# Four edits at handovers of a four-layer macaron kernel: folded matrices, the second pair's answers, choices one turn further apart, rows merged by tile

## The chip, the cores and the metric

The program runs on one core of one Trainium2 chip. The metric is the device time of that core in microseconds (us), lower is better. A core has five engines that each work through a queue of their own in order: PE (matrix products and transposes), DVE (vector work), ACT (activations and copies), POOL (here mostly small element-wise work and the indirect scatters) and SP (which issues most transfers). They meet through semaphores.

## What is computed

x has 4 batches of 512 rows of 128 numbers (2048 rows in all). It goes through four layers, each of the same shape; the two feed-forward halves of a layer share their weights:

```python
for layer in (0, 1, 2, 3):
    x = x + 0.5 * ffn[layer](layernorm(x))
    x = x + attn[layer](layernorm(x))
    x = x + 0.5 * ffn[layer](layernorm(x))
```

The feed-forward parts differ by layer:

- layer 0: a mixture of 8 experts, each row goes to one expert (relu, 512 hidden units); an expert takes the first 320 rows that chose it, later ones get nothing;
- layer 1: sigmoid gates, each row goes to its two best of 8 small experts (64 hidden units each), and to one shared expert;
- layer 2: each row goes to its two best of 8 *linear* experts, `y += gate_e * ((x @ w_in[e].T) @ w_out[e].T)`;
- layer 3: a mixture of 8 experts, each row goes to its two best (relu, 512 hidden units). An expert holds 512 rows; all first choices are ranked ahead of all second choices, so the second choices fill up what the first ones left.

Attention is causal softmax with 16 heads in layers 0 and 1, softmax without a mask in layer 3, and a gated decay over the sequence in layer 2.

## The kernel before

x stays on the chip in four tiles `xs[b]`, one per batch b, each 128 partitions by 4 tiles of 128. Batches are worked on singly or in two **pairs**, [0, 1] and [2, 3]. Many steps are written as generators that `yield` between turns; `skewed(gens, lag)` (L1519) runs several of them in rounds, where generator i joins after i x lag rounds, and so sets the order in which their instructions are written. Outside of a `manual_schedule` block a scheduler in the framework may still move instructions; inside of the one at L1639, POOL keeps the written order. On the chip each engine then takes its instructions strictly in the order of its queue.

**A mixture** (class `Mixture`; f00 and f01 are the two of layer 0, f30 and f31 the two of layer 3) has three steps.

- `tokens(bs, ...)` (L296) normalizes rows (n_f), transposes them (T_f, L195), scores them (lg_f, L330), picks the experts on DVE (from mx_f, L344, on), ranks every row within its expert by matrix products (rank_f, L373), works out addresses (kept, at, slot, to_f, L400 to L409) and has POOL copy the gates beside the rows and scatter them with indirect DMAs, 128 rows each, into one buffer per choice (`disp`, L416).
- `experts(w)` (L426) fetches, for each expert e, its rows d (first choices) and, in layer 3, d2 (second choices). `prepare(e)` (L452) clears in d2 what lies where first choices already fill the slots (a factor `behind` of 0 or 1 per slot), adds d2 to d, transposes d (dT_f, L463) and copies the transposes by ACT. Then come the two products h_f (L487) and o_f (L523), and POOL scatters the answers (L509) into `res`. A row of d or d2 has 128 numbers and 2 more, its row number and its gate.
- `combine(b)` (L533) reads the answers of batch b back (r_f, a DMA on SP's queue) and adds them to `xs[b]` on DVE. The tile r_f comes from a ring of three, tag "n", which the normalized rows of the following stage share.

**Layer 2's matrices.** As the experts of layer 2 are linear, `prep_l2` (L1296) folds w_in[e] and w_out[e] into one 128 x 128 matrix m per expert. The raw weights are fetched while f01's experts run. Then, per expert: four transposes of w_out (wo2T, L1326), a copy to SBUF, four accumulating products with w_in (L1331), a copy into m. Both copies go through the helper `copy` (L131), which alternates between DVE and ACT; in this place all wo2T copies fall to DVE and all copies into m to ACT.

**The first half of layer 1** follows. `combine` of f01 is run for all four batches (L1586), then `followed(pool, bs)` (L1592) for the two pairs, the second 12 rounds behind the first. It calls `l1_ffn(pool, 0, bs)` (L1134): statistics on DVE, rs_f, rstd_f and off_f on POOL, normalized rows n_f on DVE and ACT by turns (`norms`, L160), T_f on PE, its copy nT on ACT, scores lg on PE, two products gu of the shared expert and of one other, the choice of two experts on DVE (`chosen`, L1075, from mx_f to comb), transposes gT of comb, their copy, a DMA of the gate rows to DRAM (rows_f) and one back that spreads them (cb_f), and then per expert h on ACT and DVE, a product with the gates on POOL (L1198) and the product down on PE. For pair 0, `followed` goes on with the start of layer 1's attention.

**Layer 2 and the choices of layer 3.** `behind(pool, bs)` (L1612) runs for each pair the second half of layer 1's feed-forward, all of layer 2, and the choices of f30; the second pair joins 4 rounds later. For pair 1 the two batches' choices are themselves staggered: `skewed([f30.tokens([b], ...) for b in bs], 3)` (L1623), so batch 3 is three turns behind batch 2.

Of the kernel before, what the change touches and what calls it, by code (L numbers as in the profile page):

```python
# [9 lines left out]
FP = mybir.dt.float32  # L10
I32 = mybir.dt.int32
AF = mybir.ActivationFunctionType
ALU = mybir.AluOpType
# [4 lines left out]
P = 128  # L18
D = 128
NB, S = 4, 512  # L20
# [3 lines left out]
E = 8  # L24
# [4 lines left out]
FF = 512  # L29
NC = FF // P  # L30
W = D + 2
# [10 lines left out]
def kernel(ctx: ExitStack, tc: tile.TileContext, a: dict, out: bass.AP):  # L42
    nc = tc.nc
# [12 lines left out]
    def bank(name):  # L56
        return psum.tile([P, 512], FP, name=name, tag="bank", bufs=8)
# [14 lines left out]
    ident = const([P, P], "ident")  # L72
# [58 lines left out]
    def copy(dst, src):  # L131
        n_copies[0] += 1
        if n_copies[0] % 2:
            nc.vector.tensor_copy(dst, src)
        else:
            nc.scalar.copy(dst, src)
# [76 lines left out]
    def bc(ap, shape):  # L213
        while len(ap.shape) < len(shape):
            ap = ap.unsqueeze(len(ap.shape))
        return ap.to_broadcast(shape)
# [28 lines left out]
    class Mixture:  # L245
# [180 lines left out]
        def experts(self, w, beside=None):  # L426

            w1, b1T, w2, b2 = w
            cap, per, whole, left = self.cap, self.per, self.cap // P, self.cap % P
            with tc.tile_pool(name=f"moe_{self.tag}", bufs=2) as pool:  # L430
                if self.k == 2:

                    ps = bank(f"n1_{self.tag}")
# [7 lines left out]
                got, made = {}, {}  # L441
# [10 lines left out]
                def prepare(e):  # L452
                    tag = f"{e}_{self.tag}"
                    d = got[e, 0]
                    if self.k == 2:
                        d2 = got[e, 1]
                        nc.vector.tensor_tensor(d2, d2, bc(behind[:, e, :], [P, per, W]), ALU.mult)
                        nc.vector.tensor_tensor(d[:, :, :D], d[:, :, :D], d2[:, :, 2:], ALU.add)
                        nc.vector.tensor_tensor(d[:, :, D:], d[:, :, D:], d2[:, :, :2], ALU.add)
                    ps = bank(f"dT{tag}")  # L460
                    for s in range(per):
                        m = min(P, cap - s * P)
                        nc.tensor.transpose(ps[:, s * P : s * P + m], d[:m, s, :D], ident[:m, :m])  # L463
                    dT = pool.tile([P, cap], FP, name=f"dT{tag}", tag="dT")
                    nc.scalar.copy(dT, ps[:, :cap])  # L465

                    back = pool.tile([P, per], I32, name=f"back{tag}", tag="back", bufs=8)
                    lost = pool.tile([P, per], FP, name=f"lost{tag}", tag="lost", bufs=4)
                    nc.vector.scalar_tensor_tensor(
                        lost, d[:, :, D], 0.0, astray[:, e * per : (e + 1) * per], ALU.is_equal, ALU.mult  # L470
                    )
                    nc.vector.tensor_tensor(back, d[:, :, D], lost, ALU.add)  # L472
                    made[e] = d, dT, back
# [822 lines left out]
    def prep_l2(pool):  # L1296

        l2["gate"] = load_T(a["L2_ffn_w_gate"], E, D, "gate2T")
        l2["w_in"] = load(a["L2_attn_W_in"], [P, 2 * D], "win2")
        l2["w_out"] = load(a["L2_attn_W_out"], [P, D], "wout2")  # L1300
        l2["b_out"] = load_row(a["L2_attn_b_out"], "bout2")
        l2["b_in"] = load_T(a["L2_attn_b_in"].rearrange("(k d) -> k d", k=2), 2, D, "bin2T")
        yield

        m = pools["w"].tile([P, E, D], FP, name="m2", tag="m2")
        l2["m"] = m
        got = {}

        def fetch(e):
            wi, wo = raw[:, 0, e].rearrange("p (c d) -> p c d", d=D), raw[:, 1, e]  # L1310
            nc.sync.dma_start(wi, a["L2_ffn_w_in"][e].rearrange("(c f) d -> f c d", f=P))
            nc.sync.dma_start(wo, a["L2_ffn_w_out"][e])
            got[e] = wi, wo

        raw = pool.tile([P, 2, E, FF], FP, name="raw2", tag="raw2")
        for e in range(E):

            behind = yield
            nc.gpsimd.tensor_copy(raw[0:1, :, e, 0], behind[0:1, 0:1].to_broadcast([1, 2]))
            fetch(e)  # L1320
        yield
        for e in range(E):
            wi, wo = got[e]
            ps = bank(f"wo2T_{e}")
            for c in range(NC):
                nc.tensor.transpose(ps[:, c * P : (c + 1) * P], wo[:, c * P : (c + 1) * P], ident)  # L1326
            woT = pool.tile([P, FF], FP, name=f"wo2T_{e}", tag="woT", bufs=3)
            copy(woT, ps)
            pm = bank(f"m2_{e}")
            for c in range(NC):  # L1330
                nc.tensor.matmul(  # L1331
                    pm[:, :D], wi[:, c, :], woT[:, c * P : (c + 1) * P], start=(c == 0), stop=(c == NC - 1)
                )
            copy(m[:, e, :], pm[:, :D])

    def l2_ffn(pool, i, bs):
        tag = f"f2{i}_{bs[0]}"
# [93 lines left out]
    l3 = {}  # L1431
# [83 lines left out]
    def whole(parts):  # L1515
        for _ in parts:
            pass

    def skewed(gens, lag):  # L1519

        live = {i: g for i, g in enumerate(gens)}
        r = 0
        while live:
            for i in list(live):
                if r >= i * lag and next(live[i], "end") == "end":
                    del live[i]
            r += 1
            yield
# [46 lines left out]
    with tc.tile_pool(name="weights12", bufs=1) as mid:  # L1575
        pools["w"] = mid
        prep_l1()
        with tc.tile_pool(name="raw2", bufs=1) as pool:
            made = prep_l2(pool)
            next(made)  # L1580
            next(made)
            f01.experts(l0["w"], made.send)
            whole(made)
        first = small.tile([P, 1], FP, name="first_sigmoid", tag="first_sigmoid", bufs=1)
        nc.scalar.activation(first, l2["m"][:, 0, 0:1], AF.Sigmoid)
        for b in range(NB):  # L1586
            whole(f01.combine(b))
        with tc.tile_pool(name="ahead1", bufs=2) as ahead:
            vpads[:] = [padded(ahead, 0), None]
            begun = l1_begin(ahead)  # L1590

            def followed(pool, bs):  # L1592
                yield from l1_ffn(pool, 0, bs)
                if bs[0] == 0:

                    yield from begun[0](0)
                    for g in range(2):
                        begun[1](0, g)
                        yield
                        begun[4][0, g] = begun[2](0, g)  # L1600

            with tc.tile_pool(name="ffn10", bufs=2) as pool:
                whole(skewed([followed(pool, bs) for bs in pairs], 12))

            early = []
            with tc.tile_pool(name="gates10", bufs=1) as pool:
                l1_attn(
                    lambda _: prep_l3_ffn(xs[0]), begun,
                    lambda b: l1_early(pool, pairs[0], early) if b == 1 else iter(()),
                )  # L1610

        def behind(pool, bs):  # L1612
            yield from l1_ffn(pool, 1, bs, early if bs[0] == 0 else None)
            yield from l2_ffn(pool, 0, bs)
            yield from l2_attn(pool, bs)
            yield from l2_ffn(pool, 1, bs)
            if bs[0] == 0:

                parts = f30.tokens(bs, l3["gate"], "scalar", pool, apart=True)
                while next(parts, "end") != "end" and next(parts, "end") != "end":  # L1620
                    yield
            else:
                yield from skewed([f30.tokens([b], l3["gate"], "scalar", pool) for b in bs], 3)  # L1623

        with tc.tile_pool(name="chain", bufs=2) as pool:
            decay = pool.tile([P, S], FP, name="decay", tag="decay", bufs=1)
            nc.gpsimd.memset(decay, 0.9)
            for bs in pairs:
                l2["gates", bs[0]] = pool.tile([P, 2 * NT, P], FP, name=f"gates{bs[0]}", tag=f"gates{bs[0]}", bufs=1)
                nc.gpsimd.memset(l2["gates", bs[0]], 0.0)  # L1630

            l2["row"] = []
            for u in range(E // 4):
                flag = pool.tile([P, 1], FP, name=f"flag{u}", tag=f"flag{u}", bufs=1)
                nc.vector.tensor_reduce(flag, ident.rearrange("p (r c) -> p r c", c=SLOT)[:, :, u], AX.X, ALU.add)
                row = pool.tile([P, P], FP, name=f"row{u}", tag=f"row{u}", bufs=1)
                nc.vector.tensor_copy(row, flag.to_broadcast([P, P]))
                l2["row"].append(row)
            with tc.manual_schedule(engines={mybir.EngineType.Pool}):  # L1639
                whole(skewed([behind(pool, bs) for bs in pairs], 4))  # L1640
        pools["w"] = wpool
# [54 lines left out]
```

## Time and profile before

The time is the median of three runs. One execution was profiled; everything with a time inside the program below is from that one.

| what | value |
|---|---|
| median of 3 runs | 1515.85 us (1512.09, 1516.94, 1515.85) |
| the profiled execution: its own time, its span | 1516.03 us, 1514.3 us |
| mean granted clock of PE in it (1 is full) | 0.914 |
| busy: PE, PE weight loads | 1278.2 us (84%), 817.5 us (54%) |
| busy: DVE, ACT, POOL | 881.6 us (58%), 682.6 us (45%), 696.5 us (46%) |
| moved by DMA | 106.21 MB, 70 GB/s in the mean |

The span is the time between the first and the last instruction in the trace, in which the times of the rows below are counted; the rest of the execution's time lies around it. The rows have two forms. A row of the **chain of waits** is one link of the chain that ended last, in order of time: start in us, length in us, the engine, the operation with its line, and a count; "issue" is time in which an engine stood with nothing that the profile shows to wait for. A row of the **timeline** is one group of like instructions on one engine: start, busy time in us, engine, line, operation, result<-operands, shapes, a count, and in brackets the idle time ahead of it and what ended it. Names without their numbers: n_f can be a row of any mixture or feed-forward part, so the time tells which one it is. The table of **PE in windows of 2 us** has the window and its length, PE's busy time in it with a count of instructions, the clock that PE was granted (1.00 is full speed), the busy share of the DMA engines, and GB/s moved.

### The profile page before, as it was taken

The numbers are of one execution on the slowest core, as the hardware profiler recorded it, in microseconds if no ns is written. First come the engines' busy times: TensorE is split into PE (matmuls) and PEld (weight loads), VectorE is DVE, ScalarE is ACT, GpSimd is POOL, SyncE is SP. The second block draws the span as 40 slices with busy tenths as digits, with TensorE's granted clock in tenths as the row PEclk, the third lists the DMA queues.
The fourth block names the chain that finished last, engine by engine and source line by source line (L and its number), as shares of the span: only waits on it lengthen the run. The fifth ranks groups of instructions, "written<-read, shape, count | busy, mean of one in ns | idle before, by whom it ended". The sixth has DMA issues, their size and how long they took to land.

```text
span 1514.3 us, 28772 instructions
## 1 busy us (share of the span) xinstructions
PE 1278.2 (84%) x10645; PEld 817.5 (54%) x10645; DVE 881.6 (58%) x2893; ACT 682.6 (45%) x1431; POOL 696.5 (46%) x808
## 2 busy tenths in 40 slices
PE   4687999995968989998999878739589999998394
PEld 3464666774755656676656656627333434343273
DVE  5336777663356657777566755434287787772343
ACT  1235877871422367776621222104336555563041
POOL 5346767871533578876443112555520323202253
PEclk9898999996989999999999887759799999998597
DMA  8410240002412874241130000032114000000223
GB/s 259 104 53 22 79 171 11 9 7 78 147 36 57 230 241 151 85 142 36 38 76 1 1 0 3 29 90 85 49 42 149 9 12 5 15 1 15 78 82 108
DMA packets 100660, 106.21 MB, mean 70 GB/s; under 512 B 9084, under 2 KB 73832, under 8 KB 100520
## 3 DMA queue, kind: packets, MB, share of 16 engines
q1 hardware_dynamic: 91752, 90.11, 20.7%
q0 software_dynamic: 6656, 13.22, 2.5%
q8 instruction: 84, 1.38, 0.4%
q10 hardware_dynamic: 2112, 1.05, 0.3%
q14 instruction: 56, 0.46, 0.1%
HBM read 62.49 MB, written 41.85 MB: 69 GB/s over the span
## 4 chain that ended last, share of the span: by engine, by line
PE 66%; DVE 9%; POOL 8%; issue 7%; DMA 6%; ACT 2%; SPq 1%; POOLq 0%; ACTq 0%; DVEq 0%
PE s_a L618 13%; PE t_a L663 8%; PE h_f L487 5%; PE acc_a L757 5%; PE o_f L523 5%; PE acc_a L685 5%; PE y_f L1380 4%; PE t_a L618 3%; PE ot_a L776 2%; POOL disp_f L416 2%; POOL res_f L509 2%; PE gate_f L1397 2%; PE lg_f L330 1%; PE T_f L195 1%; DVE low L707 1%
## 5 line engine op out<-in xcount | busy, mean ns | idle before, releaser
L650 POOL TENSOR_SCALAR sc_a<-sc_a,top_a 128x128 f32<-128x128 f32 (+3 forms) x256 | 276.5, 1096 | 84.4 <-DVE top_a L635 58.5
L618 PE MATMUL s_a<-k_a,q_a 32*128 32x512 f32 (+3 forms) x1536 | 262.7, 540 | 5.4 <-DVE top_a L639 3.5
L727 ACT ACTIVATE w_a<-t_a 128x512 f32<-128x512 f32 x256 | 140.2, 595 | 124.2 <-PE t_a L618 92.1
L707 DVE TENSOR_REDUCE low<-s_a 128x1 f32<-128x512 f32 x256 | 163.4, 684 | 47.8 <-PE t_a L618 34.8
L663 PE MATMUL t_a<-ident,sc_a 128*128 128x128 f32 x1280 | 170.9, 279 | 6.1 <-DVE top_a L639 5.3
L618 PE MATMUL t_a<-ql_a,k_a 32*128 32x512 f32 x512 | 169.7, 648 | 0.5 <-DVE low L707 0.2
L509 POOL DMA_INDIRECT res_f<-y_f,back_f x112 | 109.7, 980 | 127.6 <-ACT y_f L508 91.3
L663 PEld LDWEIGHTS t_a<-ident,sc_a 128*128 128x128 f32 x1280 | 142.1, 142 | 41.2 <-issue 15.6
L652 ACT ACTIVATE sc_a<-sc_a,top_a 128x128 f32<-128x128 f32 (+3 forms) x256 | 134.8, 575 | 13.9 <-DVE top_a L639 13.4
L618 PEld LDWEIGHTS s_a<-k_a,q_a 32*128 32x128 f32 x1536 | 92.0, 185 | 77.7 <-issue 42.5
L672 ACT ACTIVATE w_a<-t_a 128x256 f32<-128x256 f32 (+2 forms) x192 | 94.3, 526 | 68.7 <-PE t_a L663 68.2
L416 POOL DMA_INDIRECT disp_f<-n_f,to_f x96 | 95.1, 991 | 55.8 <-issue 37.1
L523 PE MATMUL o_f<-w_l,h_f 128*128 128x128 f32 (+1 forms) x896 | 110.5, 278 | 1.4 <-ACT h_f L491 1.0
L523 PEld LDWEIGHTS o_f<-w_l,h_f 128*128 128x128 f32 (+1 forms) x896 | 102.3, 184 | 10.3 <-DVE back_f L472 4.4
L487 PE MATMUL h_f<-dT_f,w_l 128*128 128x320 f32 (+1 forms) x256 | 104.0, 544 | 2.8 <-ACT dT_f L465 2.8
L685 PE MATMUL acc_a<-w_a,vpad 128*32 128x128 f32 x2560 | 97.6, 278 | 0.6 <-ACT w_a L672 0.6
L674 ACT COPY w_a<-t_a 128x256 f32<-128x256 f32 (+2 forms) x192 | 93.3, 526 | 5.7 <-PE t_a L663 5.3
L172 POOL TENSOR_SCALAR rs_f<-mv_f 128x4 f32<-128x4 f32 (+1 forms) x23 | 5.3, 232 | 194.8 <-DVE mv_f L169 194.3
L639 DVE CUSTOM_DVE_ANT_0 sc_a<-s_a,future 128x128 f32<-128x128 f32 (+3 forms) x128 | 62.3, 487 | 45.0 <-PE s_a L618 41.4
L639 DVE CUSTOM_DVE_ANT_0 sc_a<-s_a,table 128x128 f32<-128x128 f32 (+3 forms) x128 | 62.5, 488 | 44.0 <-PE s_a L618 33.6
L757 PE MATMUL acc_a<-w_a,vpad 128*32 128x256 f32 x1024 | 84.8, 400 | 2.8 <-ACT w_a L727 1.9
L508 ACT ACTIVATE y_f<-o_f,d_f 128x128 f32<-128x128 f32 (+1 forms) x112 | 39.0, 394 | 103.5 <-DVE o_f L503 92.4
(344 smaller groups left out, 2227.3 us busy)
## 6 DMA issues: line engine op xcount, KB each, us to landing
fac_a<-fac_a_sb SPq DMA_DIRECT2D x36, 256.0 KB
disp_f<-zeros_f SPq DMA_DIRECT2D x4, 2080.0 KB
d_f<-disp_f SPq DMA_DIRECT2D x32, 260.0 KB
w_l<-in_L_ffn_w_dram SPq DMA_DIRECT2D x16, 512.0 KB
cb_f<-rows_f SPq DMA_DIRECT2D x16, 512.0 KB
q_a<-fac_a SPq DMA_DIRECT2D x32, 256.0 KB
k_a<-fac_a SPq DMA_DIRECT2D x32, 256.0 KB
r_f<-res_f SPq DMA_DIRECT2D x16, 256.0 KB
```

The lines of the kernel that those rows point to most:

```text
L416: nc.gpsimd.indirect_dma_start(out=self.to[c][i0 + t][:, :], out_offset=bass.IndirectOffsetOnAxis(ap=to[:, c, t : t + 1], axis=0), in_=ns[ ...
L487: nc.tensor.matmul(ps[u][:, :cap], w1[:, e, (c + u) * P : (c + u + 1) * P], dT, start=True, stop=True)
L509: nc.gpsimd.indirect_dma_start(out=self.back[e * per + s][:, :], out_offset=bass.IndirectOffsetOnAxis(ap=back[:m, s : s + 1], axis=0), in_ ...
L523: nc.tensor.matmul(po[:m, s, :], h[:, c, s * P : s * P + m], w2[:, e, c, :], start=(c == 0), stop=(c == NC - 1),)
L618: nc.tensor.matmul(ps[:, n0:n1], q[r : r + SLOT, i * P : (i + 1) * P], k[r : r + SLOT, n0:n1], start=True, stop=True)
L650: nc.gpsimd.tensor_scalar(sc, sc, top, None, ALU.subtract)
L652: nc.scalar.activation(sc, sc, AF.Exp, bias=top, scale=-1.0)
L663: nc.tensor.transpose(ps[:, x * n + j * P : x * n + (j + 1) * P], st["sc", u, i, r0 + x][:, j * P : (j + 1) * P], ident,)
L685: nc.tensor.matmul(st["acc", u][r * SLOT : (r + 1) * SLOT, i * P : (i + 1) * P], vpads[b % 2][:, j, g * 4 + r, :], st["w", u, i, r][:, j * ...
L707: nc.vector.tensor_reduce(st["low", u][:, i, c : c + 1], ps, AX.X, ALU.max, negate=True)
L727: nc.scalar.activation(w, ps, AF.Exp)
L757: nc.tensor.matmul(acc[r * SLOT : (r + 1) * SLOT, n0:n1], vpads[b % 2][:, j, g * 4 + r, :], st["w", u, j, r][:, n0:n1], start=(j == 0 and ...
```

## The change

There are four edits.

1. In `prepare`, the pass over all of d2 and the add of all of d are replaced by one fused instruction per tile of 128 rows (second row x `behind` + first row), four per expert. The two numbers beside each row are then multiplied and added for themselves.
2. In `prep_l2`, the transposes of expert e are written ahead of the products of expert e - 1, and both copies go to ACT always.
3. `combine` of f01 runs ahead of layer 1 for batches 0 and 1 only; the one for batches 2 and 3 becomes the first two turns of their own `followed`, whose lag is 10 instead of 12.
4. The two staggered choices of f30 in pair 1 are four turns apart instead of three.

```diff
--- before.py
+++ after.py
@@ -454,8 +454,11 @@
                     d = got[e, 0]
                     if self.k == 2:
                         d2 = got[e, 1]
-                        nc.vector.tensor_tensor(d2, d2, bc(behind[:, e, :], [P, per, W]), ALU.mult)
-                        nc.vector.tensor_tensor(d[:, :, :D], d[:, :, :D], d2[:, :, 2:], ALU.add)
+                        for s in range(per):
+                            nc.vector.scalar_tensor_tensor(
+                                d[:, s, :D], d2[:, s, 2:], behind[:, e, s : s + 1], d[:, s, :D], ALU.mult, ALU.add
+                            )
+                        nc.vector.tensor_tensor(d2[:, :, :2], d2[:, :, :2], bc(behind[:, e, :], [P, per, 2]), ALU.mult)
                         nc.vector.tensor_tensor(d[:, :, D:], d[:, :, D:], d2[:, :, :2], ALU.add)
                     ps = bank(f"dT{tag}")
                     for s in range(per):
@@ -1319,19 +1322,23 @@
             nc.gpsimd.tensor_copy(raw[0:1, :, e, 0], behind[0:1, 0:1].to_broadcast([1, 2]))
             fetch(e)
         yield
-        for e in range(E):
-            wi, wo = got[e]
-            ps = bank(f"wo2T_{e}")
-            for c in range(NC):
-                nc.tensor.transpose(ps[:, c * P : (c + 1) * P], wo[:, c * P : (c + 1) * P], ident)
-            woT = pool.tile([P, FF], FP, name=f"wo2T_{e}", tag="woT", bufs=3)
-            copy(woT, ps)
-            pm = bank(f"m2_{e}")
-            for c in range(NC):
-                nc.tensor.matmul(
-                    pm[:, :D], wi[:, c, :], woT[:, c * P : (c + 1) * P], start=(c == 0), stop=(c == NC - 1)
-                )
-            copy(m[:, e, :], pm[:, :D])
+
+        wT = {}
+        for e in range(E + 1):
+            if e < E:
+                ps = bank(f"wo2T_{e}")
+                for c in range(NC):
+                    nc.tensor.transpose(ps[:, c * P : (c + 1) * P], got[e][1][:, c * P : (c + 1) * P], ident)
+                wT[e] = pool.tile([P, FF], FP, name=f"wo2T_{e}", tag="woT", bufs=3)
+                nc.scalar.copy(wT[e], ps)
+            if e > 0:
+                pm = bank(f"m2_{e - 1}")
+                for c in range(NC):
+                    nc.tensor.matmul(
+                        pm[:, :D], got[e - 1][0][:, c, :], wT[e - 1][:, c * P : (c + 1) * P],
+                        start=(c == 0), stop=(c == NC - 1),
+                    )
+                nc.scalar.copy(m[:, e - 1, :], pm[:, :D])
 
     def l2_ffn(pool, i, bs):
         tag = f"f2{i}_{bs[0]}"
@@ -1583,13 +1590,16 @@
             whole(made)
         first = small.tile([P, 1], FP, name="first_sigmoid", tag="first_sigmoid", bufs=1)
         nc.scalar.activation(first, l2["m"][:, 0, 0:1], AF.Sigmoid)
-        for b in range(NB):
+        for b in pairs[0]:
             whole(f01.combine(b))
         with tc.tile_pool(name="ahead1", bufs=2) as ahead:
             vpads[:] = [padded(ahead, 0), None]
             begun = l1_begin(ahead)
 
             def followed(pool, bs):
+                if bs[0] > 0:
+                    for b in bs:
+                        yield from f01.combine(b)
                 yield from l1_ffn(pool, 0, bs)
                 if bs[0] == 0:
 
@@ -1600,7 +1610,7 @@
                         begun[4][0, g] = begun[2](0, g)
 
             with tc.tile_pool(name="ffn10", bufs=2) as pool:
-                whole(skewed([followed(pool, bs) for bs in pairs], 12))
+                whole(skewed([followed(pool, bs) for bs in pairs], 10))
 
             early = []
             with tc.tile_pool(name="gates10", bufs=1) as pool:
@@ -1620,7 +1630,7 @@
                 while next(parts, "end") != "end" and next(parts, "end") != "end":
                     yield
             else:
-                yield from skewed([f30.tokens([b], l3["gate"], "scalar", pool) for b in bs], 3)
+                yield from skewed([f30.tokens([b], l3["gate"], "scalar", pool) for b in bs], 4)
 
         with tc.tile_pool(name="chain", bufs=2) as pool:
             decay = pool.tile([P, S], FP, name="decay", tag="decay", bufs=1)
```

## The prediction

> **What bounds the kernel now.** I read the share line of the chain of waits first, then the chain in order of time at the three places that the change touches, then the timeline there, last PE's granted clock in 2 us windows.
>
> ```profile
> PE 66%; DVE 9%; POOL 8%; issue 7%; DMA 6%; ACT 2%; SPq 1%; POOLq 0%; ACTq 0%; DVEq 0%
> ...
> 438.17 0.44 PE wo2T L1326 x4
> 438.61 2.90 issue
> 441.51 1.13 PE m L1331 x8
> 442.64 1.27 PE T_f L195 x8
> ```
>
> Two thirds of the span are matrix work, which the change leaves alone (no matmul goes or comes). What it can win lies in the handovers. Here, behind the first mixture of layer 0's second half, pair 0's normalized rows end at 436.58 (last of ACT's n_f), but their transposes T_f start at 442.64, behind the last matrix product of layer 2: PE stood 2.90 us for its operand. The timeline says why:
>
> ```profile
> 432.94 1.68 POOL L173 TENSOR_TENSOR rstd_f<-rs_f,mhalf 128x8 f32<-128x8 f32 x1
> ...
> 440.47 0.34 DVE L186 TENSOR_SCALAR n_f<-x,mv_f,rstd_f 128x128 f32<-128x128 f32 x1 [2.33 <-POOL rstd_f L173]
> 440.73 0.68 DVE L134 COPY wo2T<-wo2T 128x512 f32<-128x512 f32 x1
> ```
>
> The copy of the last wo2T stands on DVE behind pair 1's n_f, which waited 2.33 us for POOL. Second place, the last two batches' choices:
>
> ```profile
> 975.89 1.63 PE L195 MATMUL T_f<-ident,n_f 128*128 128x128 f32 x4 [3.04 <-ACT n_f L182]
> 977.31 0.53 PE L373 MATMUL rank_f<-masks_f,not_before 128*128 128x64 f32 x2
> 980.35 0.19 DVE L344 TENSOR_REDUCE mx_f<-lg_f 128x4 f32<-128x32 f32 x1 [1.20 <-PE lg_f L330]
> 981.00 0.17 DVE L409 TENSOR_TENSOR to_f<-slot_f,spare_f 128x8 int32<-128x8 f32 x1
> 982.03 1.12 POOL L416 DMA_INDIRECT disp_f<-n_f,to_f  x1 [6.12 <-DVE masks_f L234]
> ```
>
> Batch 2's rank waits on PE behind batch 3's transposes, its addresses to_f on DVE behind batch 3's mx_f, and POOL, which then issues 16 scatters one after another to 1002.65, starts 6.12 us late. Third, the first expert of layer 3:
>
> ```profile
> 1008.29 0.70 DVE L457 TENSOR_TENSOR d_f<-d_f,behind_f 128x520 f32<-128x520 f32 x1 [3.07 <-DMA d_f<-disp_f]
> 1009.03 0.69 DVE L458 TENSOR_TENSOR d_f<-d_f,d_f 128x512 f32<-128x512 f32 x1
> ...
> 1010.03 1.09 PE L463 MATMUL dT_f<-ident,d_f 128*128 128x128 f32 x4 [23.26 <-DMA d_f<-disp_f]
> ```
>
> Two full passes of DVE run before PE may begin. The second mixture repeats it (1429.07, transposes at 1430.60).
>
> **Part 1: layer 2's matrices and the second pair's answers.** In the new order of instructions, DVE loses eight wo2T copies, and the adds of batches 2 and 3 move behind pair 0's n_f. Between its first add at 425.84 and its last statistic at 432.30, DVE did two of those adds and two of those copies (starts about 0.65 apart, 2.6 us) and waited 0.24 for the fourth answer: the statistics now end near 429.4. POOL needs the same 2.6 us as before (432.30 to off_f at 434.90): n_f from 432.0.
>
> ACT takes the copies: 8 at 0.59 (its nT copy has that size), beside 0.27 for each m, plus the table load of 1.28 after m 0. PE per matrix at full clock: transposes 0.44, products 0.89, so 1.4 us against 2.4 now (418.75, 421.08, 423.46), as the transposes run ahead of the copy. With the table load in front of the third copy (423.2), products 2 to 6 end near 430.7. The last copy stands on ACT behind two n_f and one m: 432.0 + 0.44 + 0.27 + 0.44 = 433.1, copy to 433.7, product 1.1, T_f at 434.85: **7.8 us earlier**.
>
> Given back: the order puts into pair 0's choices (mx at 449.34 to comb at 457.25, 7.9 us) batch 3's add (0.69), four statistics and a new wait. Counted through in that order: mx 0.22, four h products 0.69, the add, eleven steps of about 0.22 and four statistics of 0.26 reach the last mv_f at 7.0; POOL's rs, off and rstd take 2.3; pair 1's n_f stands in front of the last comb, which ends at 9.85. So +1.95, and +0.3 because four n_f of ACT (1.65) now stand before the gT copies, whose own wait hides most of them. Behind that POOL wait on DVE queue comb, three n_f and the next h products; PE waits for comb. POOL's vpad and future fills (3.3 us) now come before pair 1's rs, but end near 438.5, before its mv_f (about 447). SP's fourth answer read waits for T_f of batch 0 and lands about 3 us later (r_f reads took 2.77 to 3.33), near 438.5; the add that needs it is reached above 440. Cover about 1.7 us; every us beyond it is lost. Behind the read on SP's queue stand only the gate rows, needed later. Sum at unchanged clock: 7.6 (at nT) - 1.95 - 0.3 = **5.3**.
>
> PE's clock decides the rest:
>
> ```profile
> 440.00:442.00 2.00, 0.49 (x4) 1.00 0.00 0
> 442.00:444.00 2.00, 2.00 (x16) 0.74 0.00 0
> 444.00:446.00 2.00, 2.00 (x9) 0.50 0.03 8
> ```
>
> After the pause the clock is 0.5 until 453, and 0.5 again after the pause at 453.9. [...] By the rows, T_f to mx takes 6.9 us at half clock; at full clock the lg (1.71, 1.51) and gu pieces (1.91) halve, 2.45 less: 7.75 in all. [...] I lean to the rows: **6.0**, ends 4.3 (also the product and T_f at half clock) and 7.8. From gT on PE's queue is the old one, and PE was full from 459 to 470, so the shift goes through to the end.
>
> **Part 2: four turns apart.** Rank 2 now stands before T_f 3: it can start when masks and pre are there, 975.92, plus 0.3 for two statistics woven in; three pairs of matmuls at half clock 1.5; then kept, at, at, at, slot, to without batch 3's mx between: 1.1. to_f at about 978.4 instead of 981.17; POOL starts 2.7 earlier. The second wmixed copy (0.3) moves before batch 3's scatters: **2.4**. Batch 3 itself comes 1 us later (to_f 987.8 instead of 986.75), hidden: its scatters start at 990.4. Ends 1.8 and 2.8.
>
> **Part 3: second rows by tile.** The pass of 0.70 and the add of 0.69 become four fused instructions of 128. None is in the trace; the nearest rows are DVE's 128x128 add at 0.29 and scalar_tensor_tensor at 0.23 (128x64) and 0.69 (128x512). First tile 0.29 after landing, the others at most 0.29 apart: last at 1.16. PE starts with the first tile and needs 1.09 for four at half clock. f30: 0.29 + 0.28 (as between 1009.72 and 1010.00) + 1.09 = 1.66 after landing, against 2.83: 1.17. f31: 1.47 against 2.62: 1.15. Sum **2.3**, ends 1.2 (a fused one at 0.5) and 2.7. [...] Later experts' rows run beside PE's 7.45 us per expert: nothing. The extra 128x8 product is 0.16, off the path.
>
> **Sum.** 6.0 + 2.4 + 2.3 = 10.7. The profiled execution took 1516.03 (span 1514.3), the runs' median is 1515.85, so the base agrees: **1505.3**.
>
> **Rivals.**
> - *Part of it given back in the choices* (0.15): the POOL wait inside pair 0's chain, or the fourth read beyond its cover, costs 3 more, and the clock stays at half through T_f: part 1 gives 1.5, all 6: about 1510. For it: DVE is strictly in order there. Against: the cover counted above.
> - *Full clock at T_f* (0.15): 7.8 + 2.4 + 2.3: 1503.5.
> - *The clock gate* (0.05), slower: the longer PE pause before comb closes the gate, and PE's full stretch from 459 to 515 runs at 0.5. Half clock costs 0.5 us per us, so it decides from 21 us on; over 35 us it costs 17: 1522. [...]
> - *The change doesn't do what it says*: the order of instructions shows all four moves, so 0.02.
>
> The likeliest case has 0.63 and spans 1501.5 to 1508.5. Below 1511.3 counts as faster (0.3%, 4.5 us, about what this kernel's measurement tells from no change; its three runs span 4.9): 0.84, same 0.10, slower 0.06. The range reaches to 1499 and to 1512.
>
> **What would show it.** T_f of pair 0 about 6 us behind the last statistic and within 1 us of the last m product; ACT's wo2T at 0.59; the last comb about 10 us after mx, with one POOL wait of about 2 us; rank 2 before T_f 3, and POOL's idle before its first late scatter near 3.5 us instead of 6.12; first dT about 0.6 us after landing. It is wrong if the fourth read holds DVE, if comb trails mx by over 12 us, or if PEclk shows half speed beyond the first 5 us after gT.

## The result and the profile after

| | before | changed |
|---|---|---|
| median of 18 runs each, same chip | 1513.49 us (1509.88 to 1517.83) | 1508.36 us (1504.37 to 1513.13) |
| profiled execution, its span | 1516.03 us, 1514.3 us | 1511.83 us, 1510.1 us |
| mean granted clock of PE in it | 0.914 | 0.912 |

The ratio is 0.9959, with a 95% interval from 0.9947 to 0.9970: 6.2 us less (4.5 to 8.0, the ratio's distance from 1 times 1513.49); the two medians lie 5.1 us apart. The change is faster, and by about half of the 10.7 us forecast. The rest of this part asks which term was short.

The lines of the changed kernel that answer to those of the prediction follow. First the share line of its chain of waits:

```profile
PE 66%; DVE 10%; POOL 8%; issue 7%; DMA 6%; ACT 2%; SPq 1%; POOLq 0%; ACTq 0%; DVEq 0%
```

By shares nothing has happened; changes of this size are only seen at their places. The first place, in the chain in order of time (start, length, link):

```profile
433.94 0.40 ACT n_f L182
434.33 0.48 ACT wo2T L1333
...
434.86 1.47 PE m L1337 x8
436.32 1.71 PE T_f L195 x8
...
447.22 6.46 issue
453.68 1.87 PE gT_f L1130 x8
```

T_f follows the last matrix product directly, and that product follows the copy on ACT, as forecast. In the timeline, whose start of T_f lies 0.2 us ahead of the chain's, the first add of an answer and T_f are these, before and then in the changed kernel:

```profile
425.84 0.69 DVE L539 TENSOR_TENSOR x<-x,r_f 128x512 f32<-128x512 f32 x1 [0.94 <-DMA r_f<-res_f]
442.48 1.44 PE L195 MATMUL T_f<-ident,n_f 128*128 128x128 f32 x8
```

```profile
427.09 0.69 DVE L542 TENSOR_TENSOR x<-x,r_f 128x512 f32<-128x512 f32 x1 [6.72 <-DMA r_f<-res_f]
436.12 1.91 PE L195 MATMUL T_f<-ident,n_f 128*128 128x128 f32 x8
```

T_f starts 9.02 us after the first add (by times not rounded), against 16.64 before: 7.6 us earlier. PE then stands 6.46 us ahead of the gate transposes, where it stood 3.50 before:

```profile
457.36 1.86 PE L1127 MATMUL gT_f<-ident,comb_f 128*8 128x128 f32 x8 [3.50 <-issue]
```

The timeline of the changed kernel shows for what:

```profile
450.86 0.25 POOL L172 TENSOR_SCALAR rs_f<-mv_f 128x8 f32<-128x8 f32 x1 [11.47 <-DVE mv_f L169]
451.39 1.68 POOL L173 TENSOR_TENSOR rstd_f<-rs_f,mhalf 128x8 f32<-128x8 f32 x1
453.10 0.35 DVE L186 TENSOR_SCALAR n_f<-x,mv_f,rstd_f 128x128 f32<-128x128 f32 x1 [1.91 <-POOL rstd_f L173]
453.36 0.22 DVE L1092 TENSOR_TENSOR comb_f<-comb_f,total_f 128x64 f32<-128x64 f32 x1
```

The last step of pair 0's comb stands on DVE behind pair 1's first n_f, and that one waited 1.91 us for POOL. The second place:

```profile
975.67 0.66 PE L373 MATMUL rank_f<-masks_f,not_before 128*128 128x64 f32 x2 [2.92 <-DVE counts_f L391]
976.97 1.06 PE L195 MATMUL T_f<-ident,n_f 128*128 128x128 f32 x4
978.22 0.17 DVE L409 TENSOR_TENSOR to_f<-slot_f,spare_f 128x8 int32<-128x8 f32 x1
979.25 1.12 POOL L416 DMA_INDIRECT disp_f<-n_f,to_f  x1 [3.24 <-ACT nT_f L321]
```

Rank stands ahead of T_f, and POOL waits 3.24 us instead of 6.12. The third:

```profile
1006.19 1.14 DVE L458 SCALAR_TENSOR_TENSOR d_f<-d_f,behind_f,d_f 128x128 f32<-128x128 f32 x4 [3.64 <-DMA d_f<-disp_f]
1006.89 1.09 PE L466 MATMUL dT_f<-ident,d_f 128*128 128x128 f32 x4 [19.88 <-DMA d_f<-disp_f]
```

PE begins 0.70 us after DVE instead of 1.74.

So each part does at its place what it should. The table splits the program at points that every kernel of the study has, to see what becomes of it. Each number is a difference of two times in the timeline of one profiled execution, all of them starts but the end of the last scatter; the runs are told below. Stage A ends with these rows, before and changed:

```profile
459.01 1.14 SPq L1131 DMA_DIRECT2D rows_f<-gT_f  x2
```

```profile
455.53 0.95 SPq L1134 DMA_DIRECT2D rows_f<-gT_f  x2
```

Where five values stand in A and B, they are of before, before again, four turns alone and the two runs of rows alone, in this order; the two values of the changed kernel are of its first and second trace.

| stage (us) | this part undone | with it, in the changed kernel |
|---|---|---|
| A: first answer's add to the DMA of the gate rows | 33.17, 29.95, 30.34, 34.43, 30.07 (mean 31.6) | 28.44, 25.09 (mean 26.8) |
| B: from there to batch 2's mx_f before layer 3 | 513.92, 515.71, 514.36, 514.21, 515.40 (mean 514.7) | 517.26, 517.06 (mean 517.2) |
| C: from there to the end of the last scatter | 29.60 to 29.73 (6 traces) | 27.19, 27.18 |
| D: f30, DVE's first merge to the first h_f | 3.62 to 3.65 (5 traces) | 2.58, 2.55 |
| D: f31, the same | 3.36, 3.37 (5 traces) | 2.42, 2.42 |

A, C and the two of D won 4.8, 2.5, 1.1 and 0.9, which makes 9.3 us. Stage B, in which no instruction was changed, is 2.5 and 2.3 us longer in the two traces than the mean of the five. That leaves 6.9 us, inside the interval of the time.

### The profile page after: what moved, and what is told of

Same layout as the page of the kernel before. It is cut to its first block, busy times and chain, and to the rows that moved or that the text cites. A ratio compares the mean times of both kernels' runs of the same rounds, so it can differ in the third digit from the quotient of the medians.

```text
span 1510.1 us, 28825 instructions
## 1 busy us (share of the span) xinstructions
PE 1283.8 (85%) x10645; PEld 823.0 (55%) x10645; DVE 873.6 (58%) x2933; ACT 688.0 (46%) x1439; POOL 692.0 (46%) x808
## 4 chain that ended last, share of the span: by engine, by line
PE 66%; DVE 10%; POOL 8%; issue 7%; DMA 6%; ACT 2%; SPq 1%; POOLq 0%; ACTq 0%; DVEq 0%
PE s_a L621 13%; PE t_a L666 8%; PE h_f L490 5%; PE o_f L526 5%; PE acc_a L760 5%; PE acc_a L688 5%; PE y_f L1387 4%; PE t_a L621 3%; POOL disp_f L416 2%; PE ot_a L779 2%; POOL res_f L512 2%; PE gate_f L1404 1%; DMA cb_f<-rows_f 1%; PE lg_f L330 1%; PE T_f L195 1%
```

## The experiments

They came in three batches of four, each batch on one chip and beside runs of the kernel before on that chip; the three chips differ. A shift of one trace against another over a stretch where both run the same instructions shows how much chance there is. The expectations speak of a grid of PE's clock: in each trace the granted clock changes only at times that lie whole multiples of 3.413 us apart, with another offset in each trace. Such a time is called a grid point here; the next section has the evidence.

**The parts alone**, on one chip. The diffs are the hunks of the change.

*Matrices alone:*

```diff
-        for e in range(E):
-            wi, wo = got[e]
...
+        for e in range(E + 1):
+            if e < E:
...
+                nc.scalar.copy(wT[e], ps)
```

> Layer 2's matrices alone (transposes ahead, both copies on ACT); all four batches' answers still ahead of layer 1, lag 12. Theory A (each local gain passes to the end in full): T_f of pair 0 starts near 436.5 instead of 442.48, since DVE loses the copies but keeps the adds of batches 2 and 3; mx to comb stays near 7.9 us, so the gate transposes gT come about 6 us earlier than before, and the time falls by about 5 to 6 us (ratio 0.996 to 0.9965). Theory B (what is won ahead of layer 1 is in part given back between layer 1's attention and the choices of layer 3): the same 6 us at gT, but less than half of it left where batch 2's mx_f starts near 973, and a ratio of 0.998 or more.

Measured: ratio 0.9965 (0.9947 to 0.9983), medians 1512.95 against 1518.02. First add to gate rows' DMA 24.92 us. In the timeline of this kernel comb is not interrupted:

```profile
453.46 0.22 DVE L1088 SCALAR_TENSOR_TENSOR comb_f<-comb_f,sc_f 128x64 f32<-128x64 f32 x1
453.71 0.22 DVE L1089 TENSOR_TENSOR comb_f<-comb_f,total_f 128x64 f32<-128x64 f32 x1
```

T_f comes 7.9 us after the first add, 1.1 earlier than in the changed kernel, but for the first batch alone; mx to the gate transposes takes 8.1 us. So the matrices carry the gain of stage A by themselves, and the ratio is the one of theory A. Stage B was 516.71 here.

*Answers alone:*

```diff
-        for b in range(NB):
+        for b in pairs[0]:
             whole(f01.combine(b))
...
+                if bs[0] > 0:
+                    for b in bs:
+                        yield from f01.combine(b)
...
-                whole(skewed([followed(pool, bs) for bs in pairs], 12))
+                whole(skewed([followed(pool, bs) for bs in pairs], 10))
```

> The second pair's answers in its own parts alone, lag 10; wo2T copies stay on DVE and the products of a matrix follow its own transposes. If the two halves of part 1 are needed together (as the prediction summed them), T_f stays within 1 us of 442.5 here. If they are substitutes, the last wo2T copy no longer stands behind pair 1's n_f and T_f starts near 438, 4 to 5 us earlier; mx to comb still grows from 7.9 to about 9.9 us, so about 2.5 us are left at gT. Ratio 0.9975 to 1.0015.

Measured: 1.0001 (0.9979 to 1.0024). T_f came 14.7 us after the first add: 1.9 earlier than before, where neither 0 nor 4 to 5 had been expected. The last two copies still stand between their own transposes and products, so PE and DVE alternate to the end. First add to gate rows' DMA 28.04; PE ran at half clock for only 2.9 us of this stretch, less than in any other trace, and the last run of this section shows what that is worth.

*Four turns alone:*

```diff
-                yield from skewed([f30.tokens([b], l3["gate"], "scalar", pool) for b in bs], 3)
+                yield from skewed([f30.tokens([b], l3["gate"], "scalar", pool) for b in bs], 4)
```

> The last two batches' choices four turns apart, nothing else; everything up to 960 us is the kernel before, so a shift of this trace against before's up to there is chance (PE's granted clock) and shows how much chance there is. Both theories: batch 2's to_f comes 2.5 to 2.8 us sooner after its mx_f than the 8.07 us of before, and the last scatter 2.4 us sooner; ratio 0.9984 (2.4 us).

Measured: 0.9992 (0.9970 to 1.0015). Batch 2's mx_f to to_f took 5.46 us instead of 8.07, stage C 27.23: 2.5 us, as in the changed kernel. The time cannot confirm or deny it: the interval is 7 us wide.

*Rows by tile alone*, twice, the second time on another chip:

```diff
-                        nc.vector.tensor_tensor(d2, d2, bc(behind[:, e, :], [P, per, W]), ALU.mult)
-                        nc.vector.tensor_tensor(d[:, :, :D], d[:, :, :D], d2[:, :, 2:], ALU.add)
+                        for s in range(per):
+                            nc.vector.scalar_tensor_tensor(
+                                d[:, s, :D], d2[:, s, 2:], behind[:, e, s : s + 1], d[:, s, :D], ALU.mult, ALU.add
+                            )
+                        nc.vector.tensor_tensor(d2[:, :, :2], d2[:, :, :2], bc(behind[:, e, :], [P, per, 2]), ALU.mult)
```

> Second rows by tile alone; everything up to 1000 us is the kernel before. Landing of d to first h_f: 2.58 us in f30 instead of 3.63, 2.42 in f31 instead of 3.37, as in the changed kernel; both theories: 2.0 us, ratio 0.9987. If the extra DVE instructions of later experts cost something, less.

> Rows by tile alone, once more: the first run had 1.06 and 0.95 us less from landing to h_f and yet a ratio of 1.0016 (1.0001 to 1.0031). If that was chance of PE's clock and of the chip, 0.9987 now, and the stage lengths away from the two landings like those of the other kernels. If the edit costs something elsewhere (more DVE instructions per expert, a longer program), again 1.001 to 1.002, and the trace shows the stage.

Measured: 1.0016 (1.0001 to 1.0031), then 0.9994 (0.9973 to 1.0015). Timeline of the first:

```profile
1014.32 1.14 DVE L458 SCALAR_TENSOR_TENSOR d_f<-d_f,behind_f,d_f 128x128 f32<-128x128 f32 x4 [3.77 <-DMA d_f<-disp_f]
1014.99 1.09 PE L466 MATMUL dT_f<-ident,d_f 128*128 128x128 f32 x4 [22.86 <-DMA d_f<-disp_f]
```

Stage D was 2.55 and 2.43 in both, as in the changed kernel, so 2.0 us are won on the spot. Neither time shows them, and the first interval leaves them out; the second holds the expected 0.9987. In no stage of the two traces did I find a cost of the edit: their f30's first h_f to f31's first merge took 417.56 and 417.41 us, within the 413.3 to 419.7 of the kernels without the edit. What this part is worth in time alone stays open.

**The changed kernel without the moved answers**, and comparisons of equal programs, on a second chip. The first is the changed kernel with its third edit taken back (the diff above, reversed).

> The changed kernel without its second edit pair (answers of batches 2 and 3 stay ahead of layer 1, lag 12): matrices, four turns, rows by tile. From the first add of an answer to the gate rows' DMA the trace of before took 33.17 us, the changed kernel 28.44, matrices alone 24.92. Theory A (moving the answers costs 3.5 us there and pays nothing later): about 25 us in that stretch, and 2 to 4 us less than the changed kernel in all, ratio to before 0.993 to 0.995. Theory B (the 3.5 us are given back further on, since pair 1 comes later or PE's clock eats them): the same 25 us, but a ratio of 0.9955 to 0.997, as the changed kernel.

Measured: 0.9942 (0.9923 to 0.9961), median 1505.36 of 8 runs. First add to gate rows' DMA 25.91, stage B 514.43.

> The changed kernel once more, for a second sample of PE's clock steps, which in each trace lie on a grid of 3.41 us with another offset. Theory of chance: from the gate rows' DMA to batch 2's mx_f of layer 3 it takes 513.9 to 517.3 us, the long value only where layer 1's attention starts about 2.6 us or later behind a grid point; ratio 0.9945 to 0.9965. Theory of a systematic loss: 517 again, whatever the offset.

Measured: 0.9963 (0.9947 to 0.9980), median 1508.63 of 12 runs. First add to gate rows' DMA 25.09: here T_f to mx took 5.44 us instead of 7.32, and PE was at half clock for at most 8.2 us of the stretch instead of 16.6. Stage B was 517.06 although layer 1's attention began 2.3 us behind a grid point, so the threshold that I had read out of six traces falls. The long stage is what the theory of a systematic loss had said; the next run speaks against it.

> The kernel before once more, as a null comparison and a further sample of the clock's offset: ratio 1.000 within 0.002; from the gate rows' DMA to batch 2's mx_f 513.9 to 514.4 us unless layer 1's attention starts about 2.6 us or later behind a grid point, then about 517; T_f to mx 4.6 us at full clock or 6.9 to 7.3 at half.

Measured: 1.0004 (0.9985 to 1.0023); stage B 515.71, where 513.9 to 514.4 or 517 had been expected. So the rule from the offset falls here too, and the kernel before, too, can have a stage B that is 1.8 us longer than in its first trace. The interval is what two equal programs give: 0.2% either way is the grain of one such comparison.

On this chip leaving the answers where they were was worth 3.1 us (means 1505.45 and 1508.55, and from the spread of the runs about 2.1 either way).

**The same question on a third chip.**

> The changed kernel without the moved answers, once more, next to the changed kernel on the same chip. If the moved answers cost time, it is again faster than the changed kernel, by about 3 us (ratio to before 0.993 to 0.995 against 0.996); if the first comparison was chance, both near 0.9955.

> The changed kernel, third sample: ratio 0.9955 to 0.9965; the first add of an answer to the gate rows' DMA 25 to 28.5 us, of which mx to comb 8.5 to 10 us with DVE's wait for POOL inside; batch 2's mx_f again 1.2 to 1.6 us behind a grid point of the clock.

Measured: 0.9925 (0.9903 to 0.9947) without the moved answers, 0.9910 (0.9889 to 0.9930) for the changed kernel, medians 1487.90 and 1485.66 against 1499.12. Both ratios lie below their forecasts, the changed kernel's clearly. The sign has turned: the changed kernel is 2.4 us ahead in the means of six runs each, about 3.9 either way, so not clear of noise. First add to gate rows' DMA 26.13 and 25.17. The grid place of batch 2's mx_f was missed: 3.07 and 2.53 us behind a grid point. So the first comparison of the two was not the last word, and no version of the study is shown to beat the changed kernel.

*Copies on DVE*, from the kernel without the moved answers:

```diff
-                nc.scalar.copy(wT[e], ps)
+                nc.vector.tensor_copy(wT[e], ps)
```

> As without the moved answers, but the wo2T copies stay on DVE; only the transposes are written ahead. If it is DVE's time that counts (the prediction's 2.6 us of copies between the first add and the last statistic, and the last copy behind pair 1's n_f), half of the gain is lost: T_f about 11 us behind the first add instead of 7.9, ratio 0.9955. If it is the order on PE, the same 7.9 and 0.994.

Measured: T_f 11.9 us after the first add. Timeline:

```profile
438.53 1.11 DVE L186 TENSOR_SCALAR n_f<-x,mv_f,rstd_f 128x128 f32<-128x128 f32 x4 [2.58 <-POOL rstd_f L173]
...
439.02 2.09 PE L195 MATMUL T_f<-ident,n_f 128*128 128x128 f32 x8 [5.76 <-DVE n_f L186]
```

Now the last product is done long before (PE stood 5.76 us), and T_f waits for the statistics, which the copies on DVE push back. T_f comes 16.64 to 17.56 us after the first add with part 1 undone and 8.0 with the copies on ACT, so about 5 us are the order on PE and about 4 are DVE's time, near the half expected. In the ratio, 0.9928 (0.9909 to 0.9948), nothing of it can be seen; 0.9955 had been expected with it.

*The changed kernel without the matrices* (the first diff of this section, reversed):

> The changed kernel with layer 2's matrices as before: moved answers, four turns, rows by tile. If the matrices carry part 1, only parts 2 and 3 are left: 4.7 us, ratio 0.997; T_f about 14.7 us behind the first add, as in the run with the answers alone. If the answers alone bring what that trace showed ahead of the gates (28.0 us to the gate rows' DMA against 31.6 in the mean of five traces with part 1 undone), 0.9945.

Measured: 0.9956 (0.9938 to 0.9973), against 0.9910 with them: by the ratios the matrices are worth about 6.9 us here. The interval holds both forecasts, 0.997 and 0.9945; the trace decides. First add to gate rows' DMA took 34.34 us, as long as with part 1 undone, so the moved answers win nothing there by themselves. T_f came 16.95 us after the first add instead of the 14.7 expected. Its timeline, then that of the answers alone:

```profile
441.43 2.05 PE L1334 MATMUL m<-wo2T,raw 128*128 128x128 f32 x8 [0.83 <-issue]
443.27 1.92 PE L195 MATMUL T_f<-ident,n_f 128*128 128x128 f32 x8
```

```profile
444.31 1.13 PE L1331 MATMUL m<-wo2T,raw 128*128 128x128 f32 x8 [0.83 <-issue]
445.27 1.04 PE L195 MATMUL T_f<-ident,n_f 128*128 128x128 f32 x8
```

The same products take 2.05 us in the one and 1.13 in the other: half clock and full clock (the 1.13 us stand at a granted clock of 1.00, from 442 to 448 us; in the changed kernel's third trace, where it was 0.59 from 434 to 436 us and 0.55 from 436 to 438, they took 2.08 us). So the 28.04 us and part of the 1.9 us of the answers alone were the clock of that execution.

## Why the prediction was right in direction and too large

**Right.** What bounds the stage, and the mechanism of every part. T_f at 434.85, which is 9.0 us after the first add: measured 9.02, 9.19 and 9.63. Given back in the choices, 1.95 + 0.3: from mx to the gate rows' DMA the changed kernel took 12.09 and 10.45, against 9.67, 7.36, 9.08, 9.67 and 7.59 with part 1 undone; that is 2.6 in the means, and 2.4 between the two traces first compared. The fourth answer's read did not hold DVE. T_f and the choices together were forecast as 5.3 us less at unchanged clock, and that is what stage A shows when traces of like clock are compared:

| stage A (us) | PE at half clock for 10.5 to 20.5 us of it | for 2.9 to 8.2 us |
|---|---|---|
| part 1 undone | 33.17, 34.43 | 29.95, 30.34, 30.07 |
| changed kernel, three traces | 28.44 | 25.09, 25.17 |
| matrices without the moved answers, three traces | 24.92, 25.91, 26.13 | |
| moved answers without the matrices, two traces | 34.34 | 28.04 |

The changed kernel is 5.4 us ahead in the first column and 5.0 in the second. The moved answers win nothing without the matrices and cost about 2.8 us beside them, in this stage and at half clock; in the whole time the two chips that were asked do not agree.

Part 2 at 2.4: 2.5. Its working, 975.92 + 0.3 + 1.5 + 1.1, adds up to 978.8 and not to the 978.4 that it gives, so by its own terms 0.4 less; to_f ended 5.60 us behind mx_f, which is 978.5 when counted from before's mx_f, since rank stood 2.88 us behind mx_f where 3.29 had been counted. So the good fit owes something to luck. Part 3 at 2.3: 2.0; four fused instructions of 128 end 1.14 us after their start, where 1.16 was forecast, and PE begins before they are done, 0.70 us after their start in f30 and 0.45 in f31, as argued (0.57 was forecast for f30).

**Mis-sized: the clock at T_f, 0.7.** I credited part 1 with a share of the 2.45 us between half and full clock (the rows named for it add up to 2.57). The share, which makes 6.0 of 5.3, was an estimate, and no run shows it. T_f to mx took 7.32, 5.44 and 5.08 in three traces of the changed kernel and 6.86, 5.03, 4.57, 7.32 and 5.03 with part 1 undone: means 5.9 and 5.8, no gain. Timeline windows of PE (window, length and busy time with a count, granted clock, DMA share, GB/s), the changed kernel's first trace and then its third:

```profile
436.00:438.00 2.00, 2.00 (x11) 0.50 0.00 0
438.00:440.00 2.00, 2.00 (x10) 0.50 0.51 139
440.00:442.00 2.00, 2.00 (x6) 0.50 0.00 0
```

```profile
436.00:438.00 2.00, 2.00 (x12) 0.55 0.00 0
438.00:440.00 2.00, 1.89 (x13) 1.00 0.45 127
440.00:442.00 2.00, 2.00 (x12) 1.00 0.05 12
```

One program, two clocks. Half clock comes with the pause ahead of the last product and T_f in either (3.54 and 3.45 us, where the prediction's times, 430.7 to 433.7, make 3.0); how long it lasts differs from execution to execution, 10.24 us in the first (435.56 to 445.80) and about 3.4 in the third (434.4 to 437.8, by the windows). In the second trace of the changed kernel this pause is 2.36 us by PE's rows and was followed by half clock as well, so the lean to the rows, to half clock behind this pause, was right.

**Failed: "so the shift goes through to the end".** I had looked for cover only within the first 15 us behind the gates. In stage B about 2.4 us of the 4.8 were gone, in the first trace of the changed kernel and in the second, from another chip. Over the whole stage the length goes with the clock: of the ten traces taken before the last batch, PE was granted half clock for 62 to 67 us in the six whose stage B took 513.9 to 515.4 us, and for 71 to 74 us in the four with 515.7 to 517.3, before again (74) among them. One place where it happens is in layer 1's attention, where PE pauses for 4.9 us and then resumes at half clock; windows of PE before, then of the changed kernel:

```profile
690.00:692.00 2.00, 0.00 (x0) 1.00 0.00 0
692.00:694.00 2.00, 1.99 (x12) 0.54 0.00 0
694.00:696.00 2.00, 2.00 (x14) 0.61 0.04 8
696.00:698.00 2.00, 2.00 (x29) 1.00 0.07 16
```

```profile
688.00:690.00 2.00, 1.34 (x8) 0.54 0.00 0
690.00:692.00 2.00, 2.00 (x12) 0.50 0.04 8
692.00:694.00 2.00, 2.00 (x12) 0.50 0.04 8
694.00:696.00 2.00, 2.00 (x23) 0.76 0.03 8
```

Before, work resumed near 692 and the clock was full at 695.56. In the changed kernel it resumed near 688.7 and was full only at 694.97, about 6 us later. PE's instructions were 3.35 us early on before's when they came into this place and 1.94 us early when they left it. So 1.4 of the 3.3 us by which stage B is longer in this trace than in before's went here. About 1.8 more go in the last 20 us ahead of batch 2's mx_f, and why was not found.

Is that chance or a loss that the change brings on? The trace's records of the clock say what the lengths are: in all 14 traces every stretch at half clock but the last of each (which the record cuts off) is a whole multiple of 3.413 us, and all their edges lie within 0.01 us on one grid, with another offset in each trace. Around T_f, for one, the clock falls at 442.97 and 456.62 us and is full again at 453.21 and 460.04 before, three steps and one; in the changed kernel it falls at 435.56 and 449.21 and is full again at 445.80 and 459.45, three steps each. I had weighed the clock for the pause ahead of T_f and not for every pause behind it. What a pause costs may then hang on where in the grid PE resumes. For the place just shown, where PE resumes with gT_f, all 14 traces tell it:

| PE resumed behind a grid point (us) | from there to the first product of acc_a (us) | traces |
|---|---|---|
| 0.12, 0.37 | 5.60, 5.48 | rows alone (first), answers alone |
| 0.49, 0.51, 0.60, 0.71 | 7.09, 7.08, 7.03, 6.98 | changed again, changed, matrices alone, changed without the matrices |
| 1.00, 1.22, 1.32 | 6.84, 6.73, 6.68 | before again, changed (third chip), copies on DVE |
| 2.38, 2.53, 2.54 | 6.17, 6.09, 6.08 | rows alone (second), four turns alone, without the moved answers (third chip) |
| 3.19, 3.28 | 5.77, 5.67 | without the moved answers, before |

The offset alone sets the length, whatever the kernel: to resume 1 us later costs 0.5 us less, and between 0.37 and 0.49 it jumps by 1.6 us, where one more step of the grid at half clock begins to be paid: about 3.4 us of half clock at 0.37 (691.2 to 694.6 in the run of the answers alone, by the windows), 6.83 at 0.51 (688.15 to 694.97 in the changed kernel). So a shift that reaches this place is halved, or overturned by the jump, and the 1.4 us are no cost of an edit in itself.

Batch 2's mx_f, at the end of stage B, lay 0.9 to 1.6 us behind a grid point in all ten traces taken before the last batch. So one can count the grid points from the first answer's add to there: 161, 160, 160, 161 and 160 with part 1 undone, 160 and 159 in the changed kernel, 159 with the matrices alone and with the answers alone, 158 without the moved answers. What part 1 wins comes out there as a grid point more or less. The one-grid-point spread among equal programs shows chance; whether the change brings PE to the dear offsets more often than before did (0.51, 0.49 and 1.22 in its three traces) so few traces do not tell, and so it stays open how much of the 2.4 us is more than chance. That the time of 18 runs (8.0 us at most) lies below the 9.3 us of the places says that some of it is lost in the mean on that chip. On the third chip the changed kernel is 13.5 us faster (10.5 to 16.6), more than its places sum to; stage B was 507.00 there, and 508.20 with the answers but without the matrices. Why the gain is larger there is open.

**The base.** I subtracted from the profiled execution's 1516.03. The 18 runs show 1513.49: this execution was 2.5 us long, and in stage A it had one of the slower clocks (half clock for 12.6 us of it).

The rivals: that part is given back was the right one of the two sides, and its 1510 lies near the measured time, but by luck: the part that the traces place is lost 250 us later than the rival had it, in PE's clock and not in the wait for POOL inside the choices, which was in the sum already. The clock did not stay at half for a long stretch behind the gates: the pause ahead of them was 3.50 us before and 6.46 in the changed kernel, and the half clock that came with it lasted to 460.04 (1.0 us into the gu products) and to 459.45; from there it was full to 528.30 and 524.31. From the gate rows' DMA to the last x<-o_f of that feed-forward it took 60.2 to 61.2 us in all traces.

## What to carry to other kernels

A handover that is shortened wins at its place what the row arithmetic says, here within about 0.4 us for every term but that of the clock. Whether the gain reaches the end can depend on a pause of PE far behind it: at the one followed here through 14 traces an earlier arrival is halved or overturned by the place in the grid (0.5 us lost per us, 1.6 us at the jump). So give a gain far from the end a range of about one step of that grid (3.4 us) either way, split the traces into stages, and compare stages with those of several executions of the old kernel, and of like clock, not with one. Look for effects of 2 us in 1500 in the stage and do not ask them of the total time, whose interval was 0.2% either way for two equal programs.

## What the runs showed that I had not expected

The clock's steps, as told. Over the 18 runs of the changed kernel, time and mean granted clock go together with a correlation of -0.90.

DVE waits that came on some chips and not on another. In all ten traces taken before the last batch DVE stood among the products for the gates in layer 2's second half, its longest wait there 0.7 to 3.8 us by trace, ended by a release that the profile calls remote; in none of the four of the last batch's chip. The same program (without the moved answers) on the second and on the last of the study's chips:

```profile
946.64 1.29 DVE L1407 TENSOR_TENSOR gb_f<-gate_f,nT_f 128x512 f32<-128x512 f32 x2 [3.65 <-remote]
```

```profile
943.88 0.68 DVE L1407 TENSOR_TENSOR gb_f<-gate_f,nT_f 128x512 f32<-128x512 f32 x1
945.45 2.48 DVE L1407 TENSOR_TENSOR gb_f<-gate_f,nT_f 128x512 f32<-128x512 f32 x4 [0.89 <-PE gate_f L1404]
```

PE's products for the gates then ran at half clock on the one (0.50 from 952 to 956 us) and at full clock on the other (1.00 from 948 to 952 us), and the stretch from the end of layer 1's attention to batch 2's mx_f took 223.4 to 224.5 us there and 215.7 to 216.3 here. What holds DVE was not found. The kernel before took 1513.49, 1518.02, 1515.07 and 1499.12 us in the four sets of runs; a ratio is only worth something beside runs on the same chip.
